# Attention weighted sums: one visit with 512 queries per key chunk instead of two visits with 256

## The chip, the cores and the metric

The kernel runs on one core of one Trainium2 chip, as one program. The metric is the device time of an execution in microseconds. Before the change three runs took 4486.51, 4490.01 and 4496.32 us; their median is 4490.01 us. Engines are named as the profile names them: PE (matmul), PEld (its weight loads), DVE (vector), ACT (activation), POOL, and SP (which issues transfers).

## The reference, cut to what matters

The program computes twelve layers on x of shape (4, 1024, 128): four groups, each with a feed-forward layer, an attention layer and the feed-forward layer again. Two of the attention layers are softmax attention with 16 heads of 8 dimensions, and only they use the changed code. The first (l0_attn) is causal, the second (l1_attn) is not:

```python
scores = jnp.einsum('bhqd,bhkd->bhqk', q, k) / np.sqrt(HD)
scores = jnp.where(causal[None, None], -jnp.inf, scores)      # l0_attn alone
attn_w = jax.nn.softmax(scores, axis=-1)
attn = jnp.einsum('bhqk,bhkd->bhqd', attn_w, v)
```

The weighted sums of this text are the last line, with exp(scores) that are not yet divided; a column of ones behind each head's values gives the divisor in the same matmul.

## The kernel before, in words

**Units.** Both softmax layers go through `softmax_attention`. The work is cut into batches (b, 4), groups of four heads (g, 4; n = 4b + g counts 16 of them) and blocks of 512 queries (qb, 2). For each (n, qb) the loop at L806 goes over chunks of 128 keys: eight in l1_attn, four (qb 0) and eight (qb 1) in l0_attn. In l0_attn the chunks on the diagonal use only the queries from `off` on (512, 384, 256 or 128 of them).

**A half-step** is one pass through the loop `for pair in (1, 0)` (L810): two heads of the four. It issues on PE two score matmuls of 64 rows (L815), two more that add the rest of the sum (L820); on ACT two exponentials of 128x512 from PSUM to the tiles `es` (L827); in l0_attn on the diagonal two masks on POOL (L830). Then it takes one step of `maxima` (L620), which runs ahead for later units: two score matmuls into a `big` tile (L639), in l0_attn sometimes two with the mask (L645), and one maximum over 128x1024 on DVE (L649). Last it calls `along` (L771), which takes one entry from the queue `pending`.

**The weighted sums** are such entries. After both half-steps of a key chunk, L837 queues what `summed` returns (L731): two calls of `half`. Each has four matmuls (L742), one per head, with 32 columns of weights each, which write 32 partitions each of one accumulator `acc`. The first call takes queries 0 to 255, the second 256 to 511, so each of the next two half-steps ends with one call. For the first key chunk of a unit (kc == 0) the first call takes all queries and the second does nothing. After the last chunk `divided` (L750) copies `acc` out on DVE, turns it over on PE (L377 through `transposed`) and divides.

**PSUM.** `big` has two tiles of two banks each (L212). `sc`, `acc` and `tr` share one pool of four tiles of one bank each (L213): a half-step's two score tiles are taken from it, and `acc` holds one of the four for the whole of a unit.

**Order.** Engines work through their queues in order. The program is recorded by Python generators (a `tick` after each half-step also takes a step of the lanes: the parts of the layers before and behind, transposes, projections, the recurrence at the end of l0_attn's batches) and a scheduler then places the instructions of each engine and the semaphores between them.

Of the kernel before, what the change touches and what calls it, by code (L numbers as in the profile page):

```python
# [3 lines left out]

# [1 line left out]

# [18 lines left out]
H, HD = 16, 8  # L25
NG = 4
BLK = 512
# [167 lines left out]
class _Kernel:  # L195
# [473 lines left out]
    def softmax_attention(self, pool, behind, w, vecs, bv, causal, begin, end):  # L669
# [6 lines left out]
        nc = self.nc  # L676
# [52 lines left out]
        pending, tails = deque(), deque()  # L729

        def summed(n, kc, es, off, out, last):  # L731

            b, g = divmod(n, NG)

            def half(k):
                if kc == 0 and k == 0:
                    out.append(self.acc())
                lo, hi = max(off, k * BLK // 2), (k + 1) * BLK // 2
                if kc == 0:
                    lo, hi = off, BLK * (1 - k)  # L740
                for i in range(4 if lo < hi else 0):
                    nc.tensor.matmul(  # L742
                        out[0][32 * i : 32 * i + 32, lo:hi],
                        lhsT=self.vas[b % 2][:, kc, (4 * g + i) * (HD + 1) :][:, :32],
                        rhs=es[i][:, lo:hi], start=kc == 0, stop=last and k == 1,
                    )

            return [lambda k=k: half(k) for k in range(2)]

        def divided(n, qb, out):  # L750
            nonlocal ended
            b, g = divmod(n, NG)
            un = pool.tile([P, BLK], F32, tag="un", name="un", bufs=2)
            nc.vector.tensor_copy(un, out[0])
            yield
            ps = self.transposed([un[:, bass.ts(i, P)] for i in range(TPB)])
            heads = ps.rearrange("p (n r) -> p n r", r=32)
            rec = self.small.tile([P, 4 * TPB], F32, tag="rec", name="rec")
            nc.vector.reciprocal(rec, heads[:, :, HD])
            nc.vector.tensor_tensor(  # L760
                ats[b][:, bass.ts(qb, TPB), g * 4 * HD : (g + 1) * 4 * HD].rearrange("p t (h d) -> p t h d", d=HD),
                ps.rearrange("p (t h r) -> p t h r", h=4, r=32)[:, :, :, :HD],
                rec.rearrange("p (t h) -> p t h", h=4).unsqueeze(3).to_broadcast([P, TPB, 4, HD]),
                ALU.mult,
            )
            if g == NG - 1 and qb == nqb - 1:
                ended = b + 1
                self.beside("ends", end(b, ats.pop(b)))
            yield

        def along():  # L771

            if tails and next(tails[0], tails) is tails:
                tails.popleft()
            if pending:
                pending.popleft()()
            while pending and not callable(pending[0]):
                tails.append(pending.popleft())
# [12 lines left out]
        for n in range(B * NG):  # L791
            b, g = divmod(n, NG)
            if g == 0:
                while (b, "values") not in ready:
                    next(maxima, None)
                    yield
                ats[b] = behind.tile([P, NT, D], F32, tag="at", name="at", bufs=2)
            for qb in range(nqb):
                while (n, qb) not in done or steps < done[n, qb] + LEAD:
                    if next(maxima, maxima) is maxima:  # L800
                        break
                    yield
                at_group, out = n, []
                most, last = (t[n % len(t)] for t in (self.most, self.last))
                nk = (qb + 1) * TPB if causal else NT
                for kc in range(nk):  # L806
                    diag = causal and kc >= qb * TPB
                    off = (kc - qb * TPB) * P if diag else 0
                    es = [None] * 4
                    for pair in (1, 0):  # L810
                        keys, queries = bass.ts(kc, P), slice(qb * BLK + off, (qb + 1) * BLK)
                        scs = [self.one("sc") for _ in range(2)]
                        for j, ps in enumerate(scs):
                            of = most[64 * j : 64 * j + 64, pair]
                            nc.tensor.matmul(  # L815
                                ps[:, off:], lhsT=of[:, 1, keys], rhs=of[:, 0, queries], start=True, stop=False
                            )
                        for j, ps in enumerate(scs):
                            of = last[64 * j : 64 * j + 64]
                            nc.tensor.matmul(  # L820
                                ps[:, off:], lhsT=of[:, 1 + pair, keys], rhs=of[:, 0, queries],
                                start=False, stop=True,
                            )
                        for j, ps in enumerate(scs):
                            i = 2 * pair + j
                            es[i] = pool.tile([P, BLK], F32, tag="es", name="es", bufs=10)
                            nc.scalar.activation(es[i][:, off:], ps[:, off:], AF.Exp, scale=ISQ)  # L827
                            if diag:
                                block = es[i][:, off : off + P]
                                nc.gpsimd.affine_select(  # L830
                                    out=block, in_=block, compare_op=ALU.is_ge, fill=0.0, base=0,
                                    pattern=[[1, P]], channel_multiplier=-1,
                                )
                        next(maxima, None)
                        along()
                        yield
                    pending.extend(summed(n, kc, es, off, out, kc == nk - 1))  # L837
                pending.append(divided(n, qb, out))
        self.easy = False
        while pending or tails:  # L840
# [813 lines left out]
```

## Time and profile before

| What | Value |
|---|---|
| median of three runs | 4490.01 us |
| the profiled execution's own time | 4454.02 us |
| its span, first to last instruction | 4452.3 us |
| mean granted PE clock | 0.916 |
| PE busy | 3783.8 us (85%) |
| DVE busy | 2665.9 us (60%) |
| ACT busy | 1704.7 us (38%) |
| POOL busy | 1024.5 us (23%) |
| score matmuls L815 and L820 | 1792 records each, 394.8 and 376.5 us busy |
| matmuls of the maxima, L639 | 1792 records, 385.3 us busy |
| weighted sums L742 | 6144 records, 566.9 us busy |

l0_attn's half-steps lie between about 282 and 1130 us of the span, l1_attn's between about 1752 and 2657 us. A matmul in f32 stands in the trace as two records, so 6144 records of L742 are 3072 matmuls, or 768 calls of four. A busy PE is not a PE at its peak: matmuls of different heads run side by side. In a row of the timeline the first number is the start in us, the second how long the row's instructions took together, "x8" how many they are, and the bracket what the engine was idle for. In a row of groups the last columns are busy time, the mean of one, and idle time just before.

### The profile page before, as it was taken

The page shows a single profiled execution, that of the slowest core. Times are in us where ns is not written, and L with a number is a line of the kernel's source. Part 1 is how long each engine was busy: PE and PEld are TensorE (multiplying, and loading weights), DVE is VectorE, ACT ScalarE, POOL GpSimd, SP SyncE. Part 2 cuts the span into 40 slices and gives each one's busy share as a digit, 9 for nine tenths or more (in the row PEclk, how much of TensorE's full clock was granted, in tenths as well). Part 3 has the DMA queues.
Part 4 walks back from the last instruction along what each step waited for, and adds up shares of the span by engine and source line. Part 5 has one row for each costly group of instructions (what it writes and reads, how often), then busy time and mean ns, then how long its engine had stood idle before and what let it go on. Part 6 is the DMA issues. An engine that isn't in the chain of part 4 may idle for free. (4 is left out here: it accounts for less than half of the span.)

```text
span 4452.3 us, 59962 instructions
## 1 busy us (share of the span) xinstructions
PE 3783.8 (85%) x21360; PEld 1963.3 (44%) x21360; DVE 2665.9 (60%) x6035; ACT 1704.7 (38%) x3066; POOL 1024.5 (23%) x1334
## 2 busy tenths in 40 slices
PE   4659999999665978899989999887795978999999
PEld 3513333333344865222222338665563654444444
DVE  8657878785777446788888854535574653223201
ACT  1216454545222222566656662222231322333322
POOL 5313323222244231202020101324324142000000
PEclk8759899999876999999999999998897989999999
DMA  2011101000001553101010005434422352000000
GB/s 103 1 47 46 37 21 39 21 29 7 1 10 37 184 166 101 44 28 39 28 64 27 30 15 188 134 117 130 136 90 72 110 155 75 1 0 0 5 5 10
DMA packets 140628, 261.74 MB, mean 59 GB/s; under 512 B 25803, under 2 KB 90187, under 8 KB 139683
## 3 DMA queue, kind: packets, MB, share of 16 engines
q1 hardware_dynamic: 123939, 224.23, 15.6%
q0 software_dynamic: 16384, 33.59, 2.5%
q8 instruction: 174, 2.85, 0.3%
q14 instruction: 131, 1.07, 0.1%
HBM read 197.31 MB, written 60.42 MB: 58 GB/s over the span
## 5 line engine op out<-in xcount | busy, mean ns | idle before, releaser
L827 ACT ACTIVATE es<-sc 128x512 f32<-128x512 f32 (+3 forms) x1792 | 892.2, 549 | 576.3 <-PE sc L820 572.8
L649 DVE TENSOR_REDUCE part<-big 128x2 f32<-128x1024 f32 (+3 forms) x768 | 877.0, 1154 | 178.2 <-PE big L639 119.5
L742 PE MATMUL acc<-es,va 128*32 128x256 f32 (+2 forms) x6144 | 566.9, 411 | 4.1 <-POOL es L830 3.4
L1546 PE MATMUL big<-xT,w 128*128 128x256 f32 x1968 | 514.3, 402 | 24.1 <-DMA w<-in_l2f_w 9.8
L639 PE MATMUL big<-most 64*128 64x512 bf16 (+3 forms) x1792 | 385.3, 368 | 93.0 <-DMA most<-pieces 58.0
L1285 PE MATMUL big<-h,l3f_w 128*128 128x512 f32 x1024 | 446.6, 593 | 5.3 <-DVE h L1271 2.3
L1546 PEld LDWEIGHTS big<-xT,w 128*128 128x128 f32 x1968 | 387.1, 202 | 103.5 <-issue 35.4
L815 PE MATMUL sc<-most 64*128 64x512 bf16 (+3 forms) x1792 | 394.8, 371 | 24.8 <-ACT es L827 11.6
L361 POOL TENSOR_TENSOR ln_rs<-ln_ve,neg_half 128x4 f32<-128x4 f32 x120 | 125.8, 1049 | 1158.1 <-DVE ln_ve L360 1133.7
L1625 POOL DMA_INDIRECT y<-rows_out,rows x256 | 246.9, 965 | 564.4 <-DVE h L1555 155.2
L820 PE MATMUL sc<-last 64*128 64x512 bf16 (+3 forms) x1792 | 376.5, 365 | 0.0
L1532 PE MATMUL acc<-h,w 128*128 128x256 f32 x1304 | 342.8, 394 | 24.1 <-DVE h L1555 16.0
L1426 POOL DMA_INDIRECT rows_in<-xn,rows x256 | 249.8, 976 | 473.7 <-DVE p_to L1114 91.2
L1285 PEld LDWEIGHTS big<-h,l3f_w 128*128 128x128 f32 x1024 | 191.9, 190 | 239.1 <-issue 230.1
L830 POOL TENSOR_SCALAR_AFFINE_SELECT es<-es 128x128 f32<-128x128 f32 x512 | 171.3, 345 | 526.5 <-ACT es L827 521.2
L1532 PEld LDWEIGHTS acc<-h,w 128*128 128x128 f32 x1304 | 241.1, 197 | 67.8 <-DVE h L1555 23.7
L742 PEld LDWEIGHTS acc<-es,va 128*32 128x32 f32 x6144 | 135.7, 109 | 297.7 <-issue 242.5
L815 PEld LDWEIGHTS <-most 64*128 64x128 bf16 x1792 | 94.3, 93 | 376.2 <-issue 353.1
L1554 ACT ACTIVATE h<-big 128x512 f32<-128x512 f32 x166 | 99.1, 597 | 402.5 <-PE big L1546 394.7
L1441 ACT ACTIVATE h<-big 128x1024 f32<-128x1024 f32 x112 | 114.4, 1024 | 328.2 <-PE big L1546 238.3
L639 PEld LDWEIGHTS <-most 64*128 64x128 bf16 x1792 | 110.8, 95 | 236.1 <-issue 119.2
L1612 DVE SCALAR_TENSOR_TENSOR x<-y,weights,x 128x128 f32<-128x128 f32 x256 | 90.9, 361 | 207.0 <-DMA y<-rows_out,rows 206.0
(291 smaller groups left out, 5195.4 us busy)
## 6 DMA issues: line engine op xcount, KB each, us to landing
w<-in_l1f_w SPq DMA_DIRECT2D x86, 768.0 KB
w<-in_l2f_w SPq DMA_DIRECT2D x84, 512.0 KB
most<-pieces SPq DMA_DIRECT2D x512, 48.0 KB
xr<-rows_in SPq DMA_DIRECT2D x170, 128.0 KB
rows_out<-yr SPq DMA_DIRECT2D x163, 128.0 KB
pieces<-pieces SPq DMA_DIRECT2D x32, 384.0 KB
most<-pieces SPq DMA_DIRECT2D x256, 32.0 KB
rows_in<-zero SPq DMA_DIRECT2D x4, 1472.0 KB
```

Source lines behind the costliest of these rows:

```text
L639: nc.tensor.matmul(ps[:, j, :w], lhsT=of[:, 0, bass.ts(q, P)], rhs=of[:, 1, c : c + w], start=True, stop=not diag,)
L649: self.paced = nc.vector.tensor_reduce(to[:, pair::2, t], ps[:, :, :w], AX.X, ALU.max, negate=True)
L742: nc.tensor.matmul(out[0][32 * i : 32 * i + 32, lo:hi], lhsT=self.vas[b % 2][:, kc, (4 * g + i) * (HD + 1) :][:, :32], rhs=es[i][:, lo:hi] ...
L815: nc.tensor.matmul(ps[:, off:], lhsT=of[:, 1, keys], rhs=of[:, 0, queries], start=True, stop=False)
L820: nc.tensor.matmul(ps[:, off:], lhsT=of[:, 1 + pair, keys], rhs=of[:, 0, queries], start=False, stop=True,)
L827: nc.scalar.activation(es[i][:, off:], ps[:, off:], AF.Exp, scale=ISQ)
L830: nc.gpsimd.affine_select(out=block, in_=block, compare_op=ALU.is_ge, fill=0.0, base=0, pattern=[[1, P]], channel_multiplier=-1,)
L1285: nc.tensor.matmul(ps[:, j, :], lhsT=m[:, i * FF + (2 * pair + j) * P : i * FF + (2 * pair + j + 1) * P], rhs=hs[z][:, i, :], start=i == 0 ...
L1426: put = nc.gpsimd.indirect_dma_start(out=k.rows_in[half.h][:, :], out_offset=bass.IndirectOffsetOnAxis(ap=at, axis=0), in_=xns[t // TPB][: ...
L1532: nc.tensor.matmul(outs[j][:, :TT], lhsT=w[:, low + c * D :][:, :D], rhs=h, start=c == 0, stop=c == NC - 1)
L1546: nc.tensor.matmul(ps[:, i, :], lhsT=w[:, bass.ts(col, P)], rhs=xT, start=True, stop=True)
L1625: got = nc.gpsimd.indirect_dma_start(out=y, out_offset=None, in_=k.rows_out[half.h][:, :], in_offset=bass.IndirectOffsetOnAxis(ap=self.row ...
```

## The change

`summed` is no longer split. It is queued as one entry per key chunk and issues its four matmuls with all queries from `off` on, up to 512 at a time. The entry is taken in the first half-step (pair 1) of the next chunk; in the second half-step (pair 0) the queue is empty, except for `divided` at a unit's end.

```diff
         def summed(n, kc, es, off, out, last):
             b, g = divmod(n, NG)
-            def half(k):
-                if kc == 0 and k == 0:
-                    out.append(self.acc())
-                lo, hi = max(off, k * BLK // 2), (k + 1) * BLK // 2
-                if kc == 0:
-                    lo, hi = off, BLK * (1 - k)
-                for i in range(4 if lo < hi else 0):
-                    nc.tensor.matmul(
-                        out[0][32 * i : 32 * i + 32, lo:hi],
-                        lhsT=self.vas[b % 2][:, kc, (4 * g + i) * (HD + 1) :][:, :32],
-                        rhs=es[i][:, lo:hi], start=kc == 0, stop=last and k == 1,
-                    )
-            return [lambda k=k: half(k) for k in range(2)]
+            if kc == 0:
+                out.append(self.acc())
+            for i in range(4):
+                nc.tensor.matmul(
+                    out[0][32 * i : 32 * i + 32, off:],
+                    lhsT=self.vas[b % 2][:, kc, (4 * g + i) * (HD + 1) :][:, :32],
+                    rhs=es[i][:, off:], start=kc == 0, stop=last,
+                )
...
-                    pending.extend(summed(n, kc, es, off, out, kc == nk - 1))
+                    pending.append(partial(summed, n, kc, es, off, out, kc == nk - 1))
```

The arithmetic, the tiles, the number of buffers, and the work on ACT, DVE, POOL and the DMA queues stay the same.

## The prediction

> **What bounds the kernel now.** I read the stretches first: in the two attention stages PE is busy 92 to 96% of almost every 100 us, DVE 72 to 89%, ACT 42 to 69%. The chain that ended last only reaches back to 3710 us, so the stage itself has to be read. The timeline of PE in a quiet part of l1_attn:
>
> ```profile
> 2205.97 0.39 PE L815 MATMUL sc<-most 64*128 64x512 bf16 x2
> 2206.20 0.38 PE L820 MATMUL sc<-last 64*128 64x512 bf16 x2
> 2206.41 0.38 PE L639 MATMUL big<-most 64*128 64x512 bf16 x2
> 2206.72 0.64 PE L742 MATMUL acc<-es,va 128*32 128x256 f32 x8
> 2207.30 0.40 PE L815 MATMUL sc<-most 64*128 64x512 bf16 x2
> ```
>
> One half-step is 2207.30 - 2205.97 = 1.33 us: 0.23 (L815), 0.21 (L820), 0.31 (L639), 0.58 (sums), with no gap. PE sets the pace. But two others are close behind. DVE, when it never waits, takes 11.27 / 9 = 1.25 us per maximum:
>
> ```profile
> 2204.76 11.27 DVE L649 TENSOR_REDUCE part<-big 128x2 f32<-128x1024 f32 x9
> ```
>
> And the score banks. `acc` holds one of four one-bank tiles, so three are left, and a half-step takes two: its second score matmul must use a bank that the half-step just before has filled, and wait until that one's first exponential has read it. How long is that loop? The end of l1_attn, where no maxima are left and PE has less to do, shows it bare:
>
> ```profile
> 2644.17 0.39 PE L815 MATMUL sc<-most 64*128 64x512 bf16 x2
> 2644.39 0.38 PE L820 MATMUL sc<-last 64*128 64x512 bf16 x2
> 2644.70 0.64 PE L742 MATMUL acc<-es,va 128*32 128x256 f32 x8
> 2645.28 0.61 PE L815 MATMUL sc<-most 64*128 64x512 bf16 x2
> 2645.52 0.58 PE L820 MATMUL sc<-last 64*128 64x512 bf16 x2
> 2646.03 0.64 PE L742 MATMUL acc<-es,va 128*32 128x256 f32 x8
> 2646.61 0.39 PE L815 MATMUL sc<-most 64*128 64x512 bf16 x2
> ```
> ```profile
> 2644.87 2.16 ACT L827 ACTIVATE es<-sc 128x512 f32<-128x512 f32 x4 [0.28 <-PE sc L820]
> ```
>
> Two L815 usually take 0.39 together; the pair at 2645.28 takes 0.61, so its second one began at 2645.28 + 0.61 - 0.39 = 2645.50. The first exponential of the half-step before began at 2644.87 and lasts 0.59 (rows of one exponential in this stage): it ends at 2645.46. So from a half-step's first score matmul to the second score matmul of the next: 0.70 to the exponential, 0.59 for it, 0.04 back, **1.33 us**. The half-step of today is as long as that by its PE work alone, so the wait is hidden exactly. Two half-steps of unequal length can't both hide it.
>
> **The change, part by part.** What a visit of 512 costs stands in the trace already, because each unit's first chunk has one:
>
> ```profile
> 2322.94 1.07 PE L742 MATMUL acc<-es,va 128*32 128x512 f32 x8
> ...
> 2323.94 0.39 PE L815 MATMUL sc<-most 64*128 64x512 bf16 x2
> ```
>
> 1.00 us to the next L815, against 0.58 for 256. So a visit is about 0.15 fixed and 0.43 per 256 queries. Merging two removes 0.15. L639 before the sums takes 0.31, before another L815 0.22 (L820 to L639, both of 64 rows): another 0.09. **PE's own work** for two half-steps falls from 2.655 to 2.41 us. That is the gain the change could have: 0.245 us each, down to 2.50 (gain 0.155) at most where DVE has a maximum per half-step.
>
> Now **the order**. In the built program of after, l1_attn runs as: half-step A (scores, maxima, sums of 512), half-step B (scores, maxima, nothing), and so on. A's work on PE is 0.23 + 0.21 + 0.31 + 1.00 = 1.75, B's 0.23 + 0.21 + 0.22 = 0.66. B's scores find their banks free (A took longer than 1.33). The scores of the next A come 0.66 after B's, and their second matmul waits for B's first exponential, 1.33 after B's start: **0.67 us of PE idle.** Behind it in PE's queue stand the other scores, the maxima and the sums; nothing overtakes. After the release, does A recover anything? A natural case says no: at 2325.29 an L815 pair lasted 0.86, so its second began at 2325.76; the sums of that half-step began at 2326.51, the next L815 at 2327.08. That is 0.75 plus 0.57, as without the wait. With 512 it is 0.75 + 1.00. So
>
> two half-steps after = 1.33 + 1.75 = 3.08 us; before 2.655; **+0.43 us** per merged pair.
>
> ACT (four exponentials, 2.2 us) and DVE (two maxima, 2.5) fit in 3.08. The sums' own inputs are in time: B's second exponential ends 0.45 after the release (0.70 + 1.08 - 1.33), the sums start at 0.75.
>
> How many? In after's order l1_attn has 254 half-steps without sums; 234 of them have no other work on PE, 11 less than 0.6 us, 9 more. About 30 of the 234 follow a unit's first chunk, which was whole before. The sum for l1_attn:
> - 234 - 30 = 204 bare pairs x 0.43 = +88.
> - The 20 with other work gain at most 0.245 each: -5.
> - The 32 first chunks: before, the four transposes of the last unit's sums (0.59) lay in the B half-step and filled it (yet the next scores waited, 1.82 from B's start in the rows above); in after's order they lie in A. A = 1.75 + 0.59, B = 1.33: 3.67 against 1.75 + 1.82 = 3.57, up to 4.17 if the transposes' bank comes late. I take +6 in all.
> - The transposes of the maxima (L657) stand in the middle of the sums in after, so the first head runs alone; one head's two records cost 0.55 (2640.08 to 2640.63), as much as four heads' eight. About +1 for each of 31, but now in place of waits on DVE of the same size (2331.50 to 2332.70 before): I take 0, bounds -10 and +15.
> - Waits of PE in this stage that a slower pace hides: on transfers of `most` 19.0 us, on DVE 11.1 and 12.7. I take -15 (bounds 0 and -40).
>
> l1_attn: **+74**.
>
> l0_attn has fewer. A narrow chunk has a shorter loop: from L815 at 422.03 to the exponential at 422.45, two of 256 in 0.66, so about 0.83 for 256 and 1.11 for 384 (397.92 to 398.51, two in 0.87). In a quiet group of four heads: three pairs of full width at +0.43; the pairs at 384 and 128 about 0, at 256 +0.15 (0.79 + 0.54 and 0.83, against 0.91 + 1.10); about +0.9 for sums that now stand one half-step sooner behind masks on POOL and transposes that leave B. That is 2.2 us, for some 10 of 16 groups: +22. The other six carry the recurrence (L929, L930, two f32 matmuls in most half-steps), which fills B: they gain up to 0.245 per pair, about -7. l0_attn: **+15**, bounds -10 and +35.
>
> Sum: 74 + 15 = **+89 us**. Against the profiled execution: 4454 + 89 = 4543. The median of the runs shown lies 36 us (0.8%) higher than that execution; the same shift gives 4490 + 89 = 4579. Both stages stand on the path: the layer behind each needs its batches. After l1_attn's last sums (2656 us) PE goes on with their transposes after 0.81 us of idle, and from 2661 us with the next layer's tiles.
>
> **A page against the change.** In the tail above PE waits for a bank in every second half-step, and the granted clock there is 1.00 (2640 to 2656 us). The Trainium skill, "TensorE: Matmul & The Clock Gate", section "A second HAM failure mode: psum-queue depth-cycling", says that frequent short idles of PE while it cycles through PSUM banks can make the clock gate swing between full and half rate. The tail doesn't show that. By the page the stalls would cost clock on top; I go by the row and leave this out of the sum.
>
> **Rivals.**
> 1. *Faster*: the wait for B's bank isn't there, because the scores of the next A find a bank or because other PE work stands in B. Then a merged pair costs 2.50 (DVE's two maxima): -0.155 x 204 = -32, -5 for the filled ones, l0_attn -0.2 x 100 = -20: 4433 (4415 to 4460). For it: PE is the busiest engine and its work does fall. Against: three banks for two per half-step force one shared bank, and the tail shows the wait. It decides from the point where B holds more than 0.67 us of other work; 9 of 254 in l1_attn do.
> 2. *Same*: half of the stall is filled and the waits on DVE and transfers give the rest back; +89 shrinks to within 9 us. This needs lower bounds everywhere: 204 x 0.2 = +41, -40, -10 in l0_attn: 4481.
> 3. *Slower still*: the idle 0.67 in 3.08 brings the granted clock down. Stretches with PE busy 67 to 69% (1130 to 1500 us) show 0.78 to 0.79, but they have idle gaps of many us. From 0.97 to 0.90 over 900 us would add 65: 4644.
> 4. *It doesn't do what it says*: the built order has 1792 sums instead of 3072, and in l1_attn all are of 512. Excluded.
>
> **Chances.** Forecast 0.82, slower still 0.06, faster 0.07, same 0.05. So slower by more than 0.2% (about what a measurement of this kernel can tell from no change) 0.88, same 0.05, faster 0.07. The forecast's own range: l1_attn's pairs at 0.30 to 0.47 instead of 0.43 (61 to 96 instead of 88) with the bounds above give 4515 to 4630, and I keep that as the range.
>
> **What would show it.** L742: 3584 records instead of 6144. In the quiet stretch: an idle gap of PE or an L815 pair of over 0.9 us in every second half-step, with ACT's exponentials as what ended it; L815 two half-steps apart 3.08 us. Exponentials in pairs with unequal gaps. ACT idle in l1_attn up by the stage's growth, DVE's share there down from 85% to near 75%. The stage from 1752 to 2657 us longer by some 75 us, the stages outside of attention unchanged. It would be wrong if the pairs are 2.4 to 2.5 us apart (rival 1), or if the pairs are 3.08 but the stage grows by far less (other waits gave way), or if the clock falls.

## The result and the profile after

| | us |
|---|---|
| after, median of four runs | 4562.27 (4556.82 to 4568.53) |
| before on the same chip, median of four runs | 4491.59 (4486.51 to 4496.32) |
| ratio | 1.0148, 95% interval 1.0125 to 1.017 |
| predicted | 4579, range 4515 to 4630 |

The change makes the kernel slower by 71 us, where 89 were forecast. The profiled execution of after took 4568.53 us, its span is 4566.8 us, the mean granted clock 0.915; PE is busy 3810.0 us (83%), DVE 2676.2 (59%), ACT 1696.9 (37%), POOL 1028.5 (23%). The groups of its page that answer to those in the table of before:

```profile
L821 ACT ACTIVATE es<-sc 128x512 f32<-128x512 f32 (+3 forms) x1792 | 882.8, 550 | 627.9 <-PE sc L814 602.5
...
L809 PE MATMUL sc<-most 64*128 64x512 bf16 (+3 forms) x1792 | 471.7, 366 | 92.0 <-ACT es L821 78.1
...
L738 PE MATMUL acc<-es,va 128*32 128x512 f32 (+3 forms) x3584 | 513.8, 574 | 5.8 <-POOL es L824 3.6
```

The sums (L738, the old L742) have 3584 records instead of 6144 and cost 513.8 us of PE instead of 566.9: the work that the change was to save is saved. Against it stand two idle times, in the last columns: PE ahead of its score matmuls L809 (the old L815), 92.0 us, of which 78.1 were ended by an exponential; and ACT ahead of its exponentials, 627.9 us. In before these were 24.8 (11.6) and 576.3:

```profile
L827 ACT ACTIVATE es<-sc 128x512 f32<-128x512 f32 (+3 forms) x1792 | 892.2, 549 | 576.3 <-PE sc L820 572.8
...
L815 PE MATMUL sc<-most 64*128 64x512 bf16 (+3 forms) x1792 | 394.8, 371 | 24.8 <-ACT es L827 11.6
```

**Where the time went.** Cut at the start of the first score matmul and of the last weighted sum of each attention layer, the two profiled executions compare so (us):

| Stretch | before | after | difference | predicted |
|---|---|---|---|---|
| l0_attn | 840.3 | 860.1 | +20 | +15 |
| between the two | 629.0 | 634.2 | +5 | 0 |
| l1_attn | 904.5 | 949.8 | +45 | +74 |
| behind l1_attn | 1795.9 | 1840.5 | +45 | 0 |

The last line is not the change's. Behind l1_attn both kernels run the same code, and over all traces of this study the stretch takes 1784 to 1796 us or 1823 to 1841, whichever kernel it is: e9 and e10 below, where l1_attn has the old sums, have 1823 and 1831, and e6 and e8, with merged sums, 1787 and 1784. It goes with the chip: e1 to e4 ran on one and e5 to e8 on another, where the stretch takes 1784 to 1790 and the kernel before has medians of 4447 and 4449 us; e9 to e11 and e12 ran on two others, with 1823 to 1836 and 4495 and 4498. Each chip was used in one session, so the hour isn't excluded, and the chip of the two profiled executions isn't on record. So the two executions lie 115 us apart and the medians 71 (the median of before is 38 us above its profiled execution, that of after 6 under). The first three lines make +70. Of them the +5 between the layers is no more than that stretch differs from run to run (625.6 in e9, 626.0 in e1, 629.0 in e3, 631.1 in e12), so that it isn't shown to be the change's.

**The stall.** The timeline of PE in a quiet part of l1_attn, one pair of half-steps and the start of the next:

```profile
2442.52 0.39 PE L809 MATMUL sc<-most 64*128 64x512 bf16 x2
...
2443.18 0.38 PE L809 MATMUL sc<-most 64*128 64x512 bf16 x1
2443.87 0.37 PE L809 MATMUL sc<-most 64*128 64x512 bf16 x1 [0.31 <-ACT es L821]
...
2444.60 1.07 PE L738 MATMUL acc<-es,va 128*32 128x512 f32 x8
2445.60 0.39 PE L809 MATMUL sc<-most 64*128 64x512 bf16 x2
```

B begins at 2442.52 (scores, a maximum, no sums). At 2443.18 A's first score matmul runs; the second stands apart, at 2443.87, with 0.31 us of idle in its bracket, ended by ACT. It was ready 0.69 earlier; the bracket is smaller because the first one's 0.38 counts as busy. 2443.87 - 2442.52 = 1.35 is the loop from B's start to the free bank, and from there A needs 1.73 to the next B: 2445.60 - 2442.52 = **3.08 us**, the number of the forecast. ACT and DVE show the same pace:

```profile
2443.22 2.16 ACT L821 ACTIVATE es<-sc 128x512 f32<-128x512 f32 x4 [0.92 <-PE sc L814]
```
```profile
2443.39 2.55 DVE L650 TENSOR_REDUCE part<-big 128x2 f32<-128x1024 f32 x2 [0.53 <-PE big L640]
```

Four exponentials in one go, then 0.92 us of idle; two maxima, then 0.53 of idle. Neither fills the 3.08. Of the 255 pairs in l1_attn (each from the first score matmul of a key chunk to that of the next), 137 are 3.1 us long (to the tenth); in before 104 are 2.6 or 2.7.

**What got smaller.** PE's waits in l1_attn, in all, how often, and the longest. First before, then after:

```profile
PE big L639 <- DMA most<-pieces: 19.0, 19, 3.5
PE tr L657 <- DVE mx L654: 12.7, 28, 2.7
...
PE sc L815 <- ACT es L827: 5.7, 10, 1.6
```
```profile
PE sc L809 <- ACT es L821: 59.1, 184, 1.3
```

The wait for the exponential is ten times what it was, and the 19.0 us on transfers and 12.7 on the last maximum of a unit are gone from the top of the list (0.5 and 0.4 us are left of them): in a stage that goes slower the transfers and the last reductions of a unit are in time. The waits of L639 on other reductions stay (11.1 us before, 12.2 after).

### The profile page after: what moved, and what is told of

The parts are those of the page before. It is cut to its first block, busy times and chain, and to the rows that moved or that the text cites. A ratio compares the mean times of both kernels' runs of the same rounds, so it can differ in the third digit from the quotient of the medians.

```text
span 4566.8 us, 54865 instructions
## 1 busy us (share of the span) xinstructions
PE 3810.0 (83%) x18800; PEld 1939.3 (42%) x18800; DVE 2676.2 (59%) x6035; ACT 1696.9 (37%) x3066; POOL 1028.5 (23%) x1334
## 5 line engine op out<-in xcount | busy, mean ns | idle before, releaser
L821 ACT ACTIVATE es<-sc 128x512 f32<-128x512 f32 (+3 forms) x1792 | 882.8, 550 | 627.9 <-PE sc L814 602.5
L809 PE MATMUL sc<-most 64*128 64x512 bf16 (+3 forms) x1792 | 471.7, 366 | 92.0 <-ACT es L821 78.1
L738 PE MATMUL acc<-es,va 128*32 128x512 f32 (+3 forms) x3584 | 513.8, 574 | 5.8 <-POOL es L824 3.6
L640 PE MATMUL big<-most 64*128 64x512 bf16 (+3 forms) x1792 | 407.0, 367 | 78.1 <-DMA most<-pieces 40.2
L814 PE MATMUL sc<-last 64*128 64x512 bf16 (+3 forms) x1792 | 417.3, 363 | 0.0
L809 PEld LDWEIGHTS <-most 64*128 64x128 bf16 x1792 | 95.9, 94 | 403.5 <-issue 351.6
L640 PEld LDWEIGHTS <-most 64*128 64x128 bf16 x1792 | 126.9, 95 | 215.3 <-issue 108.2
L378 PE MATMUL tr<-ident,fp_y 128*88 128x128 f32 (+1 forms) x324 | 74.3, 391 | 158.6 <-POOL fp_y L456 158.6
L814 PEld LDWEIGHTS <-last 64*128 64x128 bf16 x1792 | 99.4, 95 | 251.9 <-issue 233.1
```

The costliest lines, as they stand in the source:

```text
L640: nc.tensor.matmul(ps[:, j, :w], lhsT=of[:, 0, bass.ts(q, P)], rhs=of[:, 1, c : c + w], start=True, stop=not diag,)
L738: nc.tensor.matmul(out[0][32 * i : 32 * i + 32, off:], lhsT=self.vas[b % 2][:, kc, (4 * g + i) * (HD + 1) :][:, :32], rhs=es[i][:, off:], ...
L809: nc.tensor.matmul(ps[:, off:], lhsT=of[:, 1, keys], rhs=of[:, 0, queries], start=True, stop=False)
L814: nc.tensor.matmul(ps[:, off:], lhsT=of[:, 1 + pair, keys], rhs=of[:, 0, queries], start=False, stop=True,)
```

## The experiments

All ratios are to the kernel before, run beside it on the same chip; a thousandth is 4.5 us. The theory: two score tiles per half-step out of three banks put a fixed loop of 1.33 us between half-steps, two halves of the sums hide it, one visit in every second half-step can't. The main rival: the merge loses to something else that is close behind PE, DVE's maxima first of all.

**e1: merged in l1_attn alone; e12: merged in l0_attn alone.** The edit of e1; in e12 both lines have `causal` in the place of `not causal`:

```diff
-                if kc == 0:
+                if kc == 0 or not causal:
                     lo, hi = off, BLK * (1 - k)
...
-                        rhs=es[i][:, lo:hi], start=kc == 0, stop=last and k == 1,
+                        rhs=es[i][:, lo:hi], start=kc == 0, stop=last and (k == 1 or not causal),
```

> Sums merged in l1_attn alone, l0_attn with two visits of 256 as before. Theory (score banks): l1_attn's quiet pairs of half-steps 3.08 us, its stage about 950 us as in the changed kernel (905 before), l0_attn's as before (841 between 282 us and its last sums); in all +45 us on before, about 4537. Rival (the loss sits in l0_attn, where sums wait for the masks on POOL): l1_attn gives nothing, total within 10 us of before.

> The complement of e1_l1_only: the kernel before with the sums merged in l0_attn alone (all key chunks), halves in l1_attn. The prediction gave l0_attn +15; the stretches of the trace of after gave it +20 and 5 more between the two attention layers; and 71 in all less the 38 of e1 leaves 33. Theory (the two parts add up and l0_attn was sized a little low): +20 to +33, ratio 1.0045 to 1.0073. Rival (most of after's loss is l1_attn's, as predicted): +15 or less, ratio 1.0033 or less.

e1: 1.0086 (1.0067 to 1.0104), +38 us; its quiet pairs are 3.08 and l1_attn takes 938.1. e12: 1.0069 (1.0048 to 1.009), +31 us; l0_attn takes 862.8. Together 69, and the whole change costs 71: the two parts add up. l1_attn costs about half of what was forecast for it, l0_attn up to twice as much.

**e2: nothing merged, the halves made unequal.** Each chunk is still taken in two visits, with 384 and 128 queries.

```diff
-                lo, hi = max(off, k * BLK // 2), (k + 1) * BLK // 2
+                lo, hi = max(off, k * 3 * P), BLK if k else 3 * P
```

> Nothing is merged: two visits per key chunk as before, but 384 and 128 queries instead of 256 and 256 (a chunk's work on PE is the same). Theory (unequal half-steps can't both hide the 1.33 us loop through three score banks): the first half-step needs 0.44 + 0.31 + 0.79 = 1.54, the second 0.44 + 0.31 + 0.37 = 1.12 and so waits until 1.33: a pair takes 2.87 instead of 2.655, L815 pairs of over 0.55 us in every second half-step, total +30 us on before (15 to 45). Rival (the loss comes from the empty half-step or from the width of 512): both half-steps have sums of under 512, so within 5 us of before, apart from 5 us for some 32 more small visits in l0_attn.

1.0082 (1.0065 to 1.0099), +36 us. PE in a quiet part:

```profile
2338.13 0.39 PE L815 MATMUL sc<-most 64*128 64x512 bf16 x2
...
2338.88 0.43 PE L742 MATMUL acc<-es,va 128*32 128x128 f32 x8
2339.24 0.61 PE L815 MATMUL sc<-most 64*128 64x512 bf16 x2
...
2340.21 0.85 PE L742 MATMUL acc<-es,va 128*32 128x384 f32 x8
2340.99 0.39 PE L815 MATMUL sc<-most 64*128 64x512 bf16 x2
```

2340.99 - 2338.13 = 2.86 instead of 2.655. No bracket shows an idle engine: the wait is the 0.61 of the pair of L815 at 2339.24 where 0.39 is usual. In l1_attn there are as many visits and as many queries, only unequal: unequal length by itself costs time. The 36 us need not all be of that kind: in the profiled execution, the fastest of its four, l1_attn is 13 us longer than in before and l0_attn 7, and l0_attn has 32 more small visits.

**e3: after, with both maxima in B.** This puts more PE work where the stall is.

```diff
-                        next(maxima, None)
+                        for _ in range(0 if pair else 2):
+                            next(maxima, None)
```

> The changed kernel with both maxima steps in the half-step without sums and none in the other. Theory: the half-step with sums loses 0.22 us of PE, the other one has 0.88 of work and still waits until 1.33; a pair takes 1.53 + 1.33 = 2.86 instead of 3.08, l1_attn's stage 20 to 45 us shorter than the changed kernel's 950, total about 4530. Rival (the loss is DVE fed in lumps): the maxima come in lumps of two, so it is slower than the changed kernel, by 20 us or more.

1.0047 (1.0026 to 1.0068): 45 us (0.0101) under after, still slower than before; l1_attn takes 910.2, 40 less than after, as forecast. The quiet pairs fall from 3.08 to 2.87, since A has one maximum less behind the wait:

```profile
2434.31 0.39 PE L809 MATMUL sc<-most 64*128 64x512 bf16 x2
...
2434.75 0.60 PE L640 MATMUL big<-most 64*128 64x512 bf16 x4
2435.18 0.85 PE L809 MATMUL sc<-most 64*128 64x512 bf16 x2
...
2437.18 0.39 PE L809 MATMUL sc<-most 64*128 64x512 bf16 x2
```

The loop in these rows: from 2434.31 to the second of the L809 that start at 2435.18 (0.85 - 0.38 later, 2435.65) is 1.34.

**e4 and e5: half of each maximum's keys, in after and in before.** Is it DVE that the merge loses to?

```diff
-                        to[:, pair::2, t], ps[:, :, :w], AX.X, ALU.max, negate=True
+                        to[:, pair::2, t], ps[:, :, 0 : w // 2], AX.X, ALU.max, negate=True
```

> The changed kernel, with each maximum taken over the first half of its keys alone, so that DVE needs about 0.7 us instead of 1.25 (left out: half of the keys in the maxima; the score matmuls for them stay). Theory: DVE is not in the loop, pairs stay at 3.08, total 0 to 15 us under the changed kernel. Rival (DVE sets the pace): l1_attn's stage shortens by 40 us or more, back to the time of before.

> The kernel before, in which each maximum is taken over the first half of its keys only (the other half is left out of the maxima), as in e4_half_reduce. Theory (the merge's cost is the bank wait, whatever DVE does): the quiet pairs of l1_attn stay at 2.66 us where those of e4 stay at 3.08, so with some 140 such pairs and the smaller effects of the first layer this kernel is 55 to 75 us under e4: a ratio of about 0.978 to 0.982 to before. Rival (what the merge loses, it loses to DVE's reductions): with these short the two orders are alike, and the ratio is that of e4, 0.9935, within 0.003.

e4 (after): 0.9935 (0.9918 to 0.9951), far more than expected, some 95 us (0.0213) under after. The total was missed, because shorter reductions shorten other stretches of both layers (l0_attn 808.7 us instead of 860.1, l1_attn 901.6 instead of 949.8). The latter is the time of before, which the rival had named as its sign; taken alone this would have looked like the rival. But the quiet pairs did not move: the timeline of PE, and DVE's reduction, now 0.69 instead of 1.25:

```profile
2396.54 0.37 PE L809 MATMUL sc<-most 64*128 64x512 bf16 x1 [0.31 <-ACT es L821]
...
2399.62 0.37 PE L809 MATMUL sc<-most 64*128 64x512 bf16 x1 [0.31 <-ACT es L821]
```
```profile
2396.05 0.69 DVE L650 TENSOR_REDUCE part<-big 128x2 f32<-128x512 f32 x1 [0.31 <-PE big L640]
```

2399.62 - 2396.54 = 3.08. The control e5 decides: before gains nearly as much from the cheap maxima (0.0191), 0.9809 (0.978 to 0.9839), and 115 of its pairs stay at 2.6 to 2.7, half-steps of 1.33:

```profile
2397.75 0.39 PE L815 MATMUL sc<-most 64*128 64x512 bf16 x2
...
2399.08 0.40 PE L815 MATMUL sc<-most 64*128 64x512 bf16 x2
```

With either speed of DVE the merged order is behind, by 0.0148 with full maxima and by 0.9935 - 0.9809 = 0.0126 with half. DVE is not what the merge loses to.

**e6 and e10: no maxima in l1_attn, in after and in before.** Now PE and DVE both have less to do. These two, and e7, e8 and e11 below, ran once each, so they are read by their traces and not by totals.

```diff
                 for pair in range(2):
+                    if not causal:
+                        yield
+                        continue
                     ps = self.big()
...
-        if not one:
+        if not causal:
+            nc.vector.memset(mx, 0.0)
+        elif not one:
```

> The kernel after, with l1_attn's maxima left out (no score matmuls of the maxima, no reductions; the maxima are set to zero). Theory: a pair of half-steps loses two lots of matmuls of the maxima. A, with the sums, has the scores and 512 queries of sums, 0.23 + 0.30 + 1.00 = 1.53 us; B has 0.45 of work but its successor's second score matmul still waits 1.33 from B's start: pair 1.53 + 1.33 = 2.86 us. The order of before has 2.44 per pair in its own stretch without maxima (2644.17 to 2646.61). If the bank were not the wall, a pair would be PE's 1.97 or ACT's four exponentials, 2.16.

> The kernel before, with l1_attn's maxima left out, the control of e6_no_maxima. Theory: the pair of its own tail, 2.44 us (2644.17 to 2646.61), against 2.87 of e6, so the merge costs the same 0.43 us per pair with the maxima gone, and l1_attn's stage is 50 to 80 us shorter than e6's 879. Rival (the merge's cost needs the maxima on PE or DVE): pairs within 0.1 of each other.

The quiet pairs are 2.87 in e6 (155 of 255 at 2.9) and 2.38 or 2.44 in e10 (117 at 2.4): 0.43 to 0.49 apart, about as with the maxima. In e6 the same bracket stands on one score matmul of each pair, 2405.20 - 2402.33 = 2.87 apart; in e10 a pair is 2465.71 - 2463.27 = 2.44:

```profile
2402.33 0.37 PE L814 MATMUL sc<-most 64*128 64x512 bf16 x1 [0.31 <-ACT es L826]
...
2405.20 0.37 PE L814 MATMUL sc<-most 64*128 64x512 bf16 x1 [0.31 <-ACT es L826]
```
```profile
2463.27 0.39 PE L820 MATMUL sc<-most 64*128 64x512 bf16 x2
...
2465.71 0.39 PE L820 MATMUL sc<-most 64*128 64x512 bf16 x2
```

The stages differ by less than expected: 879.3 in e6 and 851.1 in e10, so 28 us where 50 to 80 were expected. In e10 seven single stalls of PE, of 4 to 17 us each and 54 us together, stand in the stage, against two of 27 us together in e6; without them the stages would lie some 55 us apart. The pairs, not the stages, carry this verdict.

**e7, e8 and e11: other banks, later sums.** Without maxima the two-bank tiles are free. e7 gives them to B's scores, so that no score matmul has to wait for the half-step just before. e8 moves the sums one half-step further back as well. e11 is e8 with the halves of before.

```diff
-                        scs = [self.one("sc") for _ in range(2)]
+                        if causal or pair:
+                            scs = [self.one("sc") for _ in range(2)]
+                        else:
+                            two = self.big()
+                            scs = [two[:, j, :] for j in range(2)]
...
-                    pending.append(partial(summed, n, kc, es, off, out, kc == nk - 1))
+                    pending.extend([lambda: None] * (not causal) + [partial(summed, n, kc, es, off, out, kc == nk - 1)])
```

The last line is e8's; in e11 `along` leaves one entry in `pending` instead, to the same end.

> As e6_no_maxima, and the two score tiles of every second half-step (B, the one without sums) of l1_attn come from the two-bank tiles that the maxima do not use any more, so that no score matmul has to wait for an exponential of the half-step just before. Theory with two walls: the bank wait goes, but the next thing is late at once, the sums, which stand right behind A's scores and need B's second exponential: 0.70 + 1.08 + 0.09 = 1.87 us from B's start, and 1.00 for the sums: pair 2.87 us, no gain on e6. Theory with the bank as the only wall: the pair falls to ACT's 2.16 to 2.2 us. The bracket on the matmuls tells them apart: on the sums (ended by the exponential) in the first, none in the second.

> As e7_no_maxima_banks, and in l1_attn the sums are taken one half-step later, so that a half-step lies between the exponentials and the sums that use them. Theory with two walls: both are away now, a pair is PE's own 1.97 us or the four exponentials of ACT, 2.16 to 2.2 us. If a pair stays near 2.87, neither the bank nor the sums' input is what holds it, and the theory falls.

> As e10_before_no_maxima, with the banks of every second half-step from the two-bank tiles and the sums one half-step later, the control of e8_no_maxima_banks_late: the order of before where neither the banks nor the sums' input are late. Theory: PE's own work sets the pair, 2 x (0.23 + 0.30 + 0.58) = 2.22 us against 1.97 of e8, so that here the merge gains its 0.25 us per pair, and l1_attn's stage is some 20 to 50 us longer than the 721 of e8. If the pair is 1.97 here too, ACT or something else sets it and the merge has no gain of its own.

PE in a quiet part, where B's scores show as `big`: from one B to the next, e7 first, then e8, then e11:

```profile
2383.82 0.39 PE L818 MATMUL big<-most 64*128 64x512 bf16 x2
...
2385.18 1.55 PE L743 MATMUL acc<-es,va 128*32 128x512 f32 x8 [0.32 <-ACT es L830]
2386.66 0.39 PE L818 MATMUL big<-most 64*128 64x512 bf16 x2
```
```profile
2402.85 0.38 PE L818 MATMUL big<-most 64*128 64x512 bf16 x2
...
2404.82 0.38 PE L818 MATMUL big<-most 64*128 64x512 bf16 x2
```
```profile
2452.69 0.39 PE L824 MATMUL big<-most 64*128 64x512 bf16 x2
...
2454.91 0.39 PE L824 MATMUL big<-most 64*128 64x512 bf16 x2
```

In e7 the pair is still 2386.66 - 2383.82 = 2.84, but the bracket has moved: the score matmuls run through, and the sums wait, 0.32 for their first exponential, and then take 1.48 instead of 1.00 because the second one comes 0.5 later. It is the second wall that was forecast. In e8 both are away and a pair is 2404.82 - 2402.85 = **1.97**; in e11 it is 2454.91 - 2452.69 = **2.22**. Only here, with the banks and the sums' inputs early, does the merge bring its 0.25 us per pair. Later sums with the old banks were not run. The stages are 833.1 us in e7, 720.6 in e8 and 796.1 in e11: e7's is 46 shorter than e6's although its quiet pairs gain 0.03 each, and e11's is 75 longer than e8's, where 20 to 50 were expected (0.25 for each of 255 pairs would be 64). Again the pairs carry the verdict.

**e9: a version that tries to use this.** Before, merged only while the recurrence of l0_attn is queued, since its matmuls fill B.

```diff
+            whole = causal and bool(self.lanes["ends"])
...
-                if kc == 0:
+                if kc == 0 or whole:
...
-                        rhs=es[i][:, lo:hi], start=kc == 0, stop=last and k == 1,
+                        rhs=es[i][:, lo:hi], start=kc == 0, stop=last and (k == 1 or whole),
```

> The kernel before, with the sums merged only in those key chunks of l0_attn at which the recurrence is still queued in the lanes: there its matmuls stand in B and fill it. Theory: where B holds 0.67 us or more of other work the merge pays its 0.245 us per pair, for some 30 to 35 pairs: about 8 us under before, ratio near 0.998, at the edge of what five rounds can tell. Rival (the sums that come a half-step sooner wait for their masks on POOL, or the stage behind gives nothing on): no gain, 1.000 or up to 1.002.

0.9976 (0.9963 to 0.9989), 11 us under before: the fastest of the kernels here that leave no work out. The gain is as small as forecast, and the upper end of its interval is only 5 us under before. That it comes from the filled B isn't shown: l0_attn takes 835.6 us instead of 840.3, but in e1, e10 and e11, whose l0_attn is that of before, it takes 838.5, 835.3 and 835.5.

## Why the prediction was right, and where its sizes were off

- **The loop of 1.33 us and the pair of 3.08**: right, the pair to the hundredth, the loop (1.35 in after, 1.34 in e3) within 0.02, and for the reason given. e2 shows the wait without a merge, e6 without maxima, e4 with a fast DVE, and e8 shows it gone when banks and sums' inputs are early. One formula fits the quiet pairs with the old banks within 0.06, the loop and then the rest of the longer half-step from its second score matmul on: after 1.33 + 1.75 = 3.08; e2, e3 and e6 1.33 + 1.53 = 2.86 (measured 2.86, 2.87, 2.87); e10 1.33 + 1.11 = 2.44 (measured 2.38 or 2.44).
- **PE's own work falls by 0.245 per pair**: right; e11's 2.22 against e8's 1.97 is 0.25, or at least that, since ACT needs as long as PE in e8. Where the walls stand, none of it reaches the end.
- **l1_attn: +74 forecast, +45 in the traces (+38 in e1)**. The term that was mis-sized is the count of bare pairs at full price: 204 x 0.43 = 88, with a range of 61 to 96. The 204 were counted by what stands in PE's queue; in before only 104 pairs really took 2.6 to 2.7 us. Followed pair by pair in the order of the program, those 104 grew by 0.43 at the median, 44 us together in after and in e1, which lies outside that range, and the other 151, of which 140 were longer already, by nothing together in after and by -11 us in e1. A pair that waits anyway loses less, and some waits vanish, as the lists above say. The prediction had -14 for all but the bare pairs. "The pairs are 3.08 but the stage grows by far less" was one of its own signs of being wrong, and in part it came true.
- **The first chunks: +6 forecast, from a difference both sides of which were wrong.** The 3.57 for before is not a pair: 1.75 + 1.82 runs from A's start to the second score matmul of the next A. From first score matmul to first score matmul the same rows of before give 2325.29 - 2322.19 = 3.10:

```profile
2322.19 0.40 PE L815 MATMUL sc<-most 64*128 64x512 bf16 x2
...
2325.29 0.86 PE L815 MATMUL sc<-most 64*128 64x512 bf16 x2
```

  In after such a pair takes 3.31, not 3.67, here 2455.07 - 2451.76 (25 pairs are 3.3):

```profile
2451.76 0.39 PE L809 MATMUL sc<-most 64*128 64x512 bf16 x2
...
2452.42 0.70 PE L809 MATMUL sc<-most 64*128 64x512 bf16 x2
...
2455.07 0.39 PE L809 MATMUL sc<-most 64*128 64x512 bf16 x2
```
```profile
2452.01 0.68 DVE L748 COPY un<-acc 128x512 f32<-128x512 f32 x1
```

  A's second score matmul began at 2452.42 + 0.70 - 0.37 = 2452.75, 0.99 after B's start instead of 1.33. That fits the bank of the last unit's `acc`, which DVE's copy has read by 2452.01 + 0.68 = 2452.69; the row names no releaser. So a quiet unit loses 3.31 - 3.10 = 0.21 here, where 3.67 - 3.57 = 0.10 and an allowance were forecast: it is luck that two wrong sides left so small a difference.
- **l0_attn: +15 forecast (+22 in the bare pairs, -7 where the recurrence fills B), +20 in the trace of after, +31 in e12** (22 to 41). PE's waits of score matmuls for exponentials grew there from 5.9 to 19.1 us (22.8 in e12). Cut at every 48th record of the first score matmul, which is one group of four heads, the ten quiet groups take 373 us together in before, e1, e9, e10 and e11, 392 in after and 396 in e12. So the +22 was right in size, and in the quietest groups it is 33.1 to 35.3, the forecast 2.2. The six groups with the recurrence (the fifth and sixth, ninth and tenth, thirteenth and fourteenth) take 461 to 466 in before, e1, e10 and e11, 462 in e9, 467 in after and 465 in e12: of the forecast gain of 7 nothing can be seen. How the loss divides between full and narrow chunks, masks and transposes was not tried by itself.
- **Rivals.** Faster (1) needed B to be filled in many pairs, which l1_attn doesn't have; where l0_attn has it, no loss and no clear gain is seen. A total near zero (2) needed every term at its low bound; the bare pairs of l1_attn came near it, 44 against 41, but the other pairs gave nothing back in after, and l0_attn cost 20 where it was to give 10. Slower by the clock (3) falls: the granted clock in l1_attn is 0.97 in both. The windows by stage, whose last columns are PE's granted clock, the DMA share and GB/s, before and then after:

```profile
1752.00:2657.00 905.00, 836.25 (x7271) 256.03 (x7269) 731.70 (x1126) 584.25 (x1069) 113.38 (x102) 0.97 0.11 35
1776.00:2726.00 950.00, 855.99 (x5476) 233.73 (x5479) 739.42 (x1126) 577.96 (x1069) 113.58 (x102) 0.97 0.10 33
```

  The page of the Trainium skill that the prediction weighed ("TensorE: Matmul & The Clock Gate", section "A second HAM failure mode: psum-queue depth-cycling") would have such stalls cost clock. Here 184 idle times of PE ahead of its score matmuls, 59.1 us in all over 950 us, did not.
- **DVE and ACT.** DVE's share of l1_attn was to fall to near 75%: it is 739.42 of 950, 78%. Before had 731.70 of 905, 81%, and not the 85% of the prediction. ACT's idle time ahead of its exponentials in l1_attn grew from 274.2 to 321.8 us, by 48, about as much as the stage.
- **The range.** The bounds of the terms add up to +2 to +147, not to the stated +25 to +140; the prediction doesn't say how it came by the narrower range.

That the total came within 18 us is in part luck, since the errors in size partly cancel: by the traces 29 too much in l1_attn, 5 too little in l0_attn and 5 behind it; by e1 and e12 36 too much and 16 too little.

## What to carry to other kernels

Before merging or unbalancing steps of a pipeline, count the buffers and time the loop that makes one free (here 0.70 from matmul to exponential, 0.59 for it, 0.04 back): while a step takes more of them than its predecessor leaves over, a short step makes the next one wait for the rest of that loop, and a long step does not win it back. So work that is cut can be worth less than nothing if the cut leaves steps of unequal length. Where a stall has been found, ask what is late next: giving the scores other banks alone brought 0.03 us per pair, because the sums' own input was the next wall at nearly the same place. And price a new stall only for the pairs that really run at the old pace; those that wait for something else have paid part of it already.

## What the runs showed of the hardware that was not expected

- **Exponentials back to back take 0.49 us each, not 0.54.** The expectations for e7 and e8 worked with 2.16 for four of them. In e8 ACT runs them through at the pairs' pace, two of them every 0.99 us:

```profile
2404.02 1.09 ACT L830 ACTIVATE es<-big 128x512 f32<-128x512 f32 x2
2405.01 1.08 ACT L830 ACTIVATE es<-sc 128x512 f32<-128x512 f32 x2
```

  One alone takes 0.60, but its successor starts 0.49 after it. At 1.97 PE and ACT are then equally long, so e8's pair could not tell whether PE alone would allow less.
- **A wait can hide in a row's length.** In the rows of e2 and e3 above the stall leaves no idle bracket, only a pair of matmuls that takes 0.61 or 0.85 instead of 0.39, since two matmuls that run side by side are shown as one row and the first keeps PE busy while the second waits.
- **Stalls with no cause in the profile.** e11 and e10 show some single stalls of 4 to 17 us; in e11 some of them lie beside a run of 16 indirect gathers on POOL:

```profile
2400.60 0.58 PE L824 MATMUL sc<-most 64*128 64x512 bf16 x1 [2.82 <-issue]
...
2410.58 1.08 ACT L836 ACTIVATE es<-big 128x512 f32<-128x512 f32 x2 [7.96 <-remote]
```

  "issue" and "remote" name nothing that was late, and no run here tests what it was. Why the stretch behind l1_attn takes 1784 to 1796 us in some traces and 1823 to 1841 in others is open too, beyond that it goes with the chip.
